# A graph convolution's sums: swapped passes, three products in the sums' banks, and steps moved to ScalarE

## The chip, the cores and the metric

The program runs on one core of a Trainium2 chip. The core has TensorE (PE in the profile, its weight loads PEld), VectorE (DVE), ScalarE (ACT), GpSimd (POOL) and SyncE (SP), each with a list of instructions of its own, worked off in order, and sixteen DMA engines that move data between memory, SBUF and PSUM. The metric is the time of one execution on the device in microseconds. The kernel before took 5058.26 us, the median of three runs from 5057.69 to 5059.12.

## The reference, cut to what matters

The reference is a network of two layers over 3125 nodes of 256 features. Each layer adds a graph convolution and a linear attention mixer to x, and then a feed-forward part. The change lies in the first layer: in its convolution, in the building of the matrix that the convolution multiplies with, and in the layer norm ahead of the first feed-forward part, which begins with a graph attention.

```python
xn = layernorm(x)
# graph convolution of layer 0: W is 256 x 256, 100000 edges src -> dst
h   = xn + segment_sum(xn[src], dst)
h   = h @ W.T + b
out = (h - mean(h, axis=0)) * rsqrt(var(h, axis=0) + 1e-5) * bn_w + bn_b
# the sum with the mixer (four blocks of attention and MLP), then the first feed-forward part
x = x + out + mixer(xn)
x = x + gat_experts(layernorm(x))    # attention over 65536 other edges gates four experts
```

## The kernel before

The sum over edges is a product with a matrix of counts. The kernel builds two such matrices in memory: `A1` in bf16, the counts of the 100000 edges, and `C2` in f32, the counts of the 65536 edges of the attention. For each column of 128 edges VectorE finds the edges that name the same entry and gives the first of them their number (`prepare`, L318 to L382, with the compares at L350 and L407), and POOL adds these values into memory by an indirect DMA (`scatter`, L418). 782 such DMAs go to `A1` and 512 to `C2`, in windows within which no entry occurs twice; a window waits for the one before. The function `both` interleaves the two lists beside the mixer. What is left of the second list is kept in `tail` and is issued after the convolution's branch (L829 and L830). A scheduler that places the instructions at compile time may set an instruction ahead of others that stand before it in the code, as long as nothing that it depends on forbids it; a block that is executed on a condition is one unit for it. `tc.no_sync_barrier()` (L791) bounds this placing and makes no engine wait.

A bf16 holds whole numbers exactly up to 256. So `prepare` also keeps, for each window, the largest value in each of two classes of edges (L365 to L378): the class is found by comparing kc/N with kc/N rounded to a whole number, and the rounding is done by adding and subtracting 8388608 (L369, L370). `at_most` (L437) turns these into a bound of the largest count, and `more` (L805 to L807) says whether it is over 256. If so, `if_more()` (L823) has the matrix counted again in f32 (`recount`) and the difference added (`residue`). With these inputs the body of the branch isn't executed; every engine still reads `more` (L787), branches, and does the bookkeeping of the semaphores that the body would have raised.

The convolution (L793 to L870) has these steps.

1. `aT`, the place of the sums (128 x 6250 f32), is filled with zeros by ScalarE (L800), `less` is the identity with its sign changed (L803), and `more` is computed.
2. The split (L809 to L821): every row of xn is written as a sum of three bf16 parts, `xb`. Part 0 is a rounded copy. For each of the next two, TensorE forms the rest in PSUM: x through the identity (L818) and minus the parts so far through `less` (L820); ScalarE rounds it (L821). A tile is 128 nodes, 25 tiles; four tiles are loaded at once, in two buffers (`rows`).
3. The branch (L823 to L828), then the tail of the second list.
4. The sums (`sums`, L726): for two passes, over the groups 0 to 2 and 3 to 6 of 512 nodes (group 6 has 53), 25 row blocks of `A1` are loaded (L743) and multiplied with the three parts (L750), one PSUM bank for each group and half of the features; group 6 has one bank for both halves. The own rows are added by a product with the identity (L757). When a pass ends, `done0` adds each sum to `aT` (L833). After both halves of a group it forms two linear products with W (L838), each of four f32 matmuls into the one bank `py`, ScalarE moves each to `yT` with the bias (L840), and VectorE takes its statistics (L842).
5. Batch norm (L846 to L870): from the statistics a scale and a shift for each feature, applied by VectorE (L865); TensorE transposes `yT` (L869), VectorE adds it to `xs` (L870). The input x was added to `xs` before (L861).

The feed-forward part follows: `normed` (L176) for groups of four tiles, with statistics on VectorE (L170, L171) and the scaling on VectorE as well (L183) unless `scalar=True` (L181, ScalarE); transposes (L195), whose result goes to SBUF by VectorE and ScalarE (L201, L199) and to memory (L953); products for the attention (L957); the first experts' products among them (L229, L931). Then the attention's logits are spread over the partitions (`asb`, L985), the rows of `C2` are loaded (`cnt`, L998), ScalarE makes penalties of them (L1002), and VectorE takes the maxima (L1005).

## Time and profile before

| what | us |
|---|---|
| median of three runs | 5058.26 |
| the profiled execution | 5066.09 |
| its span | 5064.4 |
| TensorE busy (matmuls) | 4018.7 (79%) |
| VectorE busy | 3209.6 (63%) |
| POOL busy | 2734.7 (54%) |
| ScalarE busy | 1499.4 (30%) |
| scatters into A (L418), 782 | 1224.7 busy, 1.566 each |
| scatters into C (L418), 512 | 794.2 busy, 1.551 each |
| last scatter into A starts | 2178.2 |
| last scatter into C starts | 2611.9 |
| split, first weights to last part | 2251.8 to 2291.7 |
| sums (L750), first to last matmul | 2324.7 to 2545 |
| batch norm's scaling (L865), first to last start | 2567.4 to 2581.1 |

The profile is of one execution, taken by the hardware. Busy times are sums over the span; whether an engine's time counts is seen only within its stage, by what the next instruction waits for. The rows of the table that have two times are from the span's start, so that the stages can be laid in order. A line of a timeline has the start, the length, the engine, the line of the code, the operation, what is written and read, how many instructions were merged, and in brackets the idle time of the engine ahead of it with what ended it. An engine with a q behind its name is its sequencer, which reads the list, branches and issues DMAs.

### The profile page before, as it was taken

The page shows a single profiled execution, that of the slowest core. Times are in us where ns is not written, and L with a number is a line of the kernel's source. Part 1 is how long each engine was busy: PE and PEld are TensorE (multiplying, and loading weights), DVE is VectorE, ACT ScalarE, POOL GpSimd, SP SyncE. Part 2 cuts the span into 40 slices and gives each one's busy share as a digit, 9 for nine tenths or more (in the row PEclk, how much of TensorE's full clock was granted, in tenths as well). Part 3 has the DMA queues.
Part 4 walks back from the last instruction along what each step waited for, and adds up shares of the span by engine and source line. Part 5 has one row for each costly group of instructions (what it writes and reads, how often), then busy time and mean ns, then how long its engine had stood idle before and what let it go on. Part 6 is the DMA issues. An engine that isn't in the chain of part 4 may idle for free. (4 is left out here: it accounts for less than half of the span.)

```text
span 5064.4 us, 50451 instructions
## 1 busy us (share of the span) xinstructions
PE 4018.7 (79%) x16771; PEld 2309.4 (46%) x16771; DVE 3209.6 (63%) x8299; ACT 1499.4 (30%) x2396; POOL 2734.7 (54%) x1835
## 2 busy tenths in 40 slices
PE   1477788878866786787979974766689998999999
PEld 1254455545633454453445642222345444454477
DVE  7978887888788879510048996889973031332231
ACT  0322133113211131130014448989740021000033
POOL 2578888888888888866740006888620031001034
PEclk6668887888777788888989986788899999999999
DMA  9934443444433323236546543323291212222176
GB/s 330 284 47 70 73 74 46 69 70 66 50 17 26 34 9 17 8 25 111 74 88 229 181 132 115 102 83 93 77 282 54 85 49 72 56 60 70 51 180 169
DMA packets 446886, 472.09 MB, mean 93 GB/s; under 512 B 213041, under 2 KB 354138, under 8 KB 441557
## 3 DMA queue, kind: packets, MB, share of 16 engines
q1 hardware_dynamic: 249418, 455.15, 29.5%
q0 software_dynamic: 197184, 13.47, 12.8%
q8 instruction: 140, 2.29, 0.2%
q14 instruction: 144, 1.18, 0.1%
HBM read 338.77 MB, written 130.63 MB: 93 GB/s over the span
## 5 line engine op out<-in xcount | busy, mean ns | idle before, releaser
L418 POOL DMA_INDIRECT A<-lowa,keya x782 | 1224.7, 1566 | 369.4 <-issue 219.0
L418 POOL DMA_INDIRECT C<-valb,keyb x512 | 794.2, 1551 | 220.9 <-issue 136.7
L1092 POOL TENSOR_TENSOR ex<-ex,pqb 128x1024 f32<-128x1024 f32 (+3 forms) x200 | 366.7, 1855 | 514.2 <-ACT ex L1091 514.0
L350 DVE SCALAR_TENSOR_TENSOR junk<-kr,keya,w_before 128x640 bf16<-128x640 f32 (+2 forms) x729 | 603.4, 828 | 14.7 <-DMA kr<-keys_a 3.3
L195 PE MATMUL tr<-ident,rows 128*128 128x128 f32 (+1 forms) x500 | 106.9, 369 | 506.8 <-ACT rows L181 488.7
L407 DVE SCALAR_TENSOR_TENSOR junk<-kr,keyb,w_before 128x1024 bf16<-128x1024 f32 (+1 forms) x390 | 496.2, 1272 | 17.0 <-DMA kr<-keys_b 11.0
L229 PE MATMUL mm<-hT,w 128*128 128x512 f32 (+1 forms) x896 | 423.0, 638 | 17.3 <-ACT hT L197 14.9
L750 PE MATMUL ag<-chb,Hb 128*128 128x512 bf16 (+1 forms) x1800 | 418.9, 386 | 12.3 <-DMA chb<-A 12.3
L750 PE MATMUL ag<-chb,xb 128*128 128x512 bf16 (+2 forms) x1950 | 399.6, 364 | 34.5 <-DMA chb<-A 34.0
L1005 DVE CUSTOM_DVE_ANT_0 am<-asb,pen 128x1664 f32<-128x1664 f32 (+3 forms) x200 | 357.2, 1786 | 48.0 <-ACT pen L1002 38.0
L707 PE MATMUL o<-w,hid 128*128 128x256 f32 (+1 forms) x1600 | 382.8, 393 | 0.0
L1127 PE MATMUL pa<-ex,hgp 128*32 128x512 f32 (+3 forms) x1400 | 217.6, 703 | 190.7 <-DVE ex L1115 187.4
L1115 DVE SCALAR_TENSOR_TENSOR ex<-ex,ct 128x2048 f32<-128x2048 f32 (+3 forms) x175 | 346.0, 2006 | 24.6 <-ACT ex L1108 14.1
L1108 ACT ACTIVATE ex<-ex,as 128x1024 f32<-128x1024 f32 (+3 forms) x400 | 344.8, 932 | 0.0
L707 PEld LDWEIGHTS o<-w,hid 128*128 128x128 f32 (+1 forms) x1600 | 296.9, 190 | 79.4 <-issue 36.9
L1358 POOL DMA_INDIRECT slots<-rb,r_ati x50 | 49.9, 998 | 513.0 <-DVE rb L1351 404.4
L232 ACT ACTIVATE hid<-mm,fm 128x512 f32<-128x512 f32 (+1 forms) x336 | 210.9, 631 | 372.1 <-PE mm L229 360.3
L195 PEld LDWEIGHTS tr<-ident,rows 128*128 128x128 f32 (+1 forms) x500 | 67.6, 178 | 551.4 <-ACT rows L181 521.7
L229 PEld LDWEIGHTS mm<-hT,w 128*128 128x128 f32 x896 | 193.1, 234 | 238.5 <-issue 195.7
L750 PEld LDWEIGHTS <-xb 128*128 128x128 bf16 (+1 forms) x2100 | 182.9, 97 | 252.1 <-issue 41.8
L750 PEld LDWEIGHTS <-Hb 128*128 128x128 bf16 (+1 forms) x2100 | 184.5, 99 | 225.5 <-issue 33.2
L181 ACT ACTIVATE rows<-xs,ln_nmr,rs_y 128x256 f32<-128x256 f32 (+1 forms) x200 | 105.2, 591 | 612.5 <-DVE ln_nmr L174 585.2
(441 smaller groups left out, 6754.9 us busy)
## 6 DMA issues: line engine op xcount, KB each, us to landing
C<-zero SPq DMA_DIRECT2D x25, 1528.0 KB
cnt<-C SPq DMA_DIRECT2D x24, 1562.5 KB
cd<-C SPq DMA_DIRECT2D x36, 1024.0 KB
kr<-keys_b SPq DMA_DIRECT2D x64, 512.0 KB
f1w<-in_f_w_dram SPq DMA_DIRECT2D x56, 512.0 KB
slots<-blank SPq DMA_DIRECT2D x15, 1820.0 KB
kr<-keys_a SPq DMA_DIRECT2D x48, 512.0 KB
kr<-keys_a SPq DMA_DIRECT2D x69, 320.0 KB
```

The lines of the kernel that those rows point to most:

```text
L229: T.matmul(ph[:, :n], lhsT=w1[:, k, hb * P:(hb + 1) * P], rhs=xT[:, k, :n], start=(k == 0), stop=(k == 1))
L232: S.activation(h[:, :n], ph[:, :n], AF.Gelu, bias=bias[hb])
L350: V.scalar_tensor_tensor(junk[:, :k * P], self.kr[:, at:at + k * P], key[:, c + j:c + j + 1], self.w_before[:, u:u + k * P], op0=OP.is_equ ...
L407: V.scalar_tensor_tensor(out, kk, key[:, c + j:c + j + 1], by, op0=OP.is_equal, op1=OP.mult, accum_out=more[:, j:j + 1] if i else self.val ...
L418: s = G.indirect_dma_start(out=self.flat, out_offset=bass.IndirectOffsetOnAxis(ap=self.idx[:, c:c + 1], axis=0), in_=(self.val if self.low ...
L707: T.matmul(po[:r], lhsT=hid[hb][:, j * P:j * P + r], rhs=w2[:, hb, :], start=(hb == 0), stop=False)
L750: T.matmul(acc[fb, g][:, :n], lhsT=Xb[:r, s, i, fb * P:(fb + 1) * P], rhs=ch[:r, at:at + n], start=first, stop=last, skip_group_check=g == ...
L1005: V.tensor_tensor_reduce(out=junk[:r, :w], in0=asb[:r, h, c0:c1], in1=pen[:r, :w], scale=1.0, scalar=-3.0e38, op0=OP.subtract, op1=OP.max, ...
L1092: G.tensor_tensor(e, e, pq[:r, h, :n], op=OP.add)
L1108: S.activation(ex[:r, h, :n], ex[:r, h, :n], AF.Exp, bias=sc)
L1115: V.scalar_tensor_tensor(e4, e4, 1.0, ct[:r, None, :m].to_broadcast([r, 4, m]), op0=OP.min, op1=OP.mult)
L1127: T.matmul(pa[32 * h:32 * h + 32, c:c + m], lhsT=hgp[:r, at:at + 32], rhs=ex[:r, h, c:c + m], start=(s == 0), stop=(s == NT - 1))
```

## The change

- The two rounding steps of the classes (L369, L370) are done by ScalarE, as copies with a scale and a bias.
- `at_most` uses PSUM banks with the tag `tr`, which the mixer has, and the bound is computed within the mixer: in the last block, ahead of the second group from the end (group 5). `more` is allocated earlier for it.
- The split forms the rest once for each tile. ScalarE rounds it to part 1, and VectorE subtracts part 1 from the rest in PSUM, which gives part 2. The rest has six banks and not five. `aT` is filled after the split in the code.
- The passes of the sums are swapped: groups 3 to 6 first, then 0 to 2. A linear product of the groups 0 to 2 goes to the bank that held this group's sum (`ag{hb}_{g}`), and no longer to `py`; the groups 3 to 6 still use `py`.
- Batch norm's scaling (L865) and the scaling of the layer norm ahead of the feed-forward part (L950) are done by ScalarE.

```diff
@@ -366,8 +366,8 @@
                 assert n * win == w and self.windows <= MOSTW
                 part = small.tile([P, COLS], F32, name="e_part", tag="e_part", bufs=1)
-                V.tensor_scalar(part[:, :w], kc, 1.0 / N, 8388608.0, op0=OP.mult, op1=OP.add)
-                V.tensor_scalar(part[:, :w], part[:, :w], -8388608.0, None, op0=OP.add)
+                S.activation(part[:, :w], kc, AF.Copy, scale=1.0 / N, bias=8388608.0)
+                S.activation(part[:, :w], part[:, :w], AF.Copy, bias=-8388608.0)
                 V.scalar_tensor_tensor(part[:, :w], kc, 1.0 / N, part[:, :w], op0=OP.mult, op1=OP.is_ge)
                 V.tensor_tensor(rel[:, :w], sel[:, :w], val, op=OP.mult)
                 V.tensor_tensor(part[:, :w], part[:, :w], rel[:, :w], op=OP.mult)
@@ -438,13 +438,13 @@
             top = small.tile([P, 2, 2], F32, name="e_top", tag="e_top")
             V.memset(top, 0.0)
-            q = ps.tile([P, P], F32, name="mq", tag="mq", bufs=1)
             for j in range(2):
                 for i in range(2):
                     n = min(P, MOSTW - i * P)
-                    p = ps.tile([P, P], BF16, name="mt", tag="mt", bufs=2)
-                    T.transpose(p[:n], self.most[:, j, i * P:i * P + n], ident_b)
-                    V.tensor_reduce(top[:n, i, j:j + 1], p[:n], axis=AX.X, op=OP.max)
+                    p = ps.tile([P, 1024], BF16, name="mt", tag="tr", bufs=2)
+                    T.transpose(p[:n, :P], self.most[:, j, i * P:i * P + n], ident_b)
+                    V.tensor_reduce(top[:n, i, j:j + 1], p[:n, :P], axis=AX.X, op=OP.max)
+            q = ps.tile([P, 512], F32, name="mq", tag="tr", bufs=2)
             for i in range(2):
                 T.matmul(q[:1, :2], lhsT=ones_col, rhs=top[:, i, :], start=(i == 0), stop=(i == 1))
             return q[:1, :2]
@@ -499,6 +499,7 @@
                 tail.append((c, (c - c0) % TAIL == TAIL - 1 or c == eb.made - 1))
+    more = ctile([1, 1], "more", I32)
     edge_stack = ExitStack()
     ep = edge_stack.enter_context(tc.tile_pool(name="ep", bufs=1, side="right"))
     with ExitStack() as st:
@@ -686,6 +687,11 @@
                 ts = tiles_of(g)
                 r = rows_of(ts[-1])
                 n = cols_of(g)
+                if l == LAYERS - 1 and g == NG - 2:
+                    assert ea.made == ea.width
+                    most = small.tile([1, 1], F32, name="most", tag="most")
+                    V.tensor_reduce(most, ea.at_most(ps), axis=AX.X, op=OP.max)
+                    V.tensor_scalar(more, most, MOST, None, op0=OP.is_gt)
                 qT = work.tile([P, 2, 512], F32, name="qT", tag="hT")
                 transposed(ps, qT, [Q[:r, t, :] for t in ts], r)
                 for j, t in enumerate(ts):
@@ -789,7 +795,6 @@
     tc.no_sync_barrier()
-    more = ctile([1, 1], "more", I32)
     with ExitStack() as st:
         gp = st.enter_context(tc.tile_pool(name="gnn0", bufs=1))
         wg = gp.tile([P, 2, D], F32, name="wg", tag="wg")
@@ -797,14 +802,10 @@
         aT = gp.tile([P, 2, N], F32, name="aT", tag="aT")
         yT = gp.tile([P, 2, N], F32, name="yT", tag="yT")
         stats = gp.tile([P, 2, NG, 6], F32, name="stats", tag="stats")
-        S.activation(aT, ones_col[:, 0:1, None].to_broadcast([P, 2, N]), AF.Copy, scale=0.0)
         xb = gp.tile([P, NT, 3, D], BF16, name="xb", tag="xb")
         less = gp.tile([P, P], BF16, name="less", tag="less")
         S.activation(less, ident, AF.Copy, scale=-1.0)
         with tc.tile_pool(name="ps_g0p", bufs=1, space=PSUM) as ps:
-            most = small.tile([1, 1], F32, name="most", tag="most")
-            V.tensor_reduce(most, ea.at_most(ps), axis=AX.X, op=OP.max)
-            V.tensor_scalar(more, most, MOST, None, op0=OP.is_gt)
             for t in range(NT):
                 r = rows_of(t)
@@ -813,12 +814,12 @@
                     load_rows(xg, xn_d, t // 4)
                 x = xg[:r, t % 4, :]
                 S.activation(xb[:r, t, 0, :], x, AF.Copy)
-                for i in range(2):
-                    p = ps.tile([P, D], F32, name="rest", tag="rest", bufs=5)
-                    T.matmul(p[:r], lhsT=ident[:r, :r], rhs=x, start=True, stop=False)
-                    for k in range(i + 1):
-                        T.matmul(p[:r], lhsT=less[:r, :r], rhs=xb[:r, t, k, :], start=False, stop=(k == i))
-                    S.activation(xb[:r, t, i + 1, :], p[:r], AF.Copy)
+                p = ps.tile([P, D], F32, name="rest", tag="rest", bufs=6)
+                T.matmul(p[:r], lhsT=ident[:r, :r], rhs=x, start=True, stop=False)
+                T.matmul(p[:r], lhsT=less[:r, :r], rhs=xb[:r, t, 0, :], start=False, stop=True)
+                S.activation(xb[:r, t, 1, :], p[:r], AF.Copy)
+                V.tensor_tensor(xb[:r, t, 2, :], p[:r], xb[:r, t, 1, :], op=OP.subtract)
+        S.activation(aT, ones_col[:, 0:1, None].to_broadcast([P, 2, N]), AF.Copy, scale=0.0)
         with (tc.tile_pool(name="g0t", bufs=1) as rp, tc.tile_pool(name="ps_g0t", bufs=1, space=PSUM) as ps,
               if_more()):
             def add0(g, fb, p, n):
@@ -833,7 +834,9 @@
                 V.tensor_tensor(aT[:, fb, 512 * g:512 * g + n], aT[:, fb, 512 * g:512 * g + n], p[:, :n], op=OP.add)
                 if fb:
                     for hb in range(2):
-                        py = ps.tile([P, 512], F32, name="py", tag="py", bufs=1)
+
+                        tag = f"ag{hb}_{g}" if g < 3 else "py"
+                        py = ps.tile([P, 512], F32, name="py", tag=tag, bufs=1)
                         for k in range(2):
                             T.matmul(py[:, :n], lhsT=wg[:, k, hb * P:(hb + 1) * P],
                                      rhs=aT[:, k, 512 * g:512 * g + n], start=(k == 0), stop=(k == 1))
@@ -841,7 +844,7 @@
                                      bias=fcol("gnn_b", hb))
                         V.bn_stats(stats[:, hb, g, :], yT[:, hb, 512 * g:512 * g + n])
-            sums(ps, gp, xb, 2, [[0, 1, 2], [3, 4, 5, 6]], done0, shared=NG - 1, own=ident_b)
+            sums(ps, gp, xb, 2, [[3, 4, 5, 6], [0, 1, 2]], done0, shared=NG - 1, own=ident_b)
         with tc.tile_pool(name="ps_g0b", bufs=1, space=PSUM) as ps:
             mv = small.tile([P, 2, 2], F32, name="bn_mv", tag="bn_mv")
             for hb in range(2):
@@ -862,7 +865,7 @@
                                 op=OP.add)
                 for hb in range(2):
                     y = yT[:, hb, 512 * g:512 * g + n]
-                    V.tensor_scalar(y, y, sc[:, hb:hb + 1], sh[:, hb:hb + 1], op0=OP.mult, op1=OP.add)
+                    S.activation(y, y, AF.Identity, scale=sc[:, hb:hb + 1], bias=sh[:, hb:hb + 1])
                 for j, t in enumerate(ts):
                     p = ps.tile([P, D], F32, name="trb", tag="trb", bufs=4)
                     for hb in range(2):
@@ -947,7 +950,7 @@
                 ts = tiles_of(g)
                 r = rows_of(ts[-1])
                 nx = work_rows(len(ts), r)
-                normed(nx, [xs[:r, t, :] for t in ts], r)
+                normed(nx, [xs[:r, t, :] for t in ts], r, scalar=True)
                 hT = work.tile([P, 2, 512], F32, name="hT", tag="hT")
                 transposed(ps, hT, nx, r)
                 nc.sync.dma_start(xf_d[:, :, 512 * g:512 * g + cols_of(g)], hT[:, :, :cols_of(g)])
```

## The prediction

> **What bounds the kernel now.** I read the chain of waits first. The 195 longest pieces that it lists all lie after 4222 us and belong to stages that the change leaves alone, so it prices nothing here. I then took the engines by stage from the end of the mixer (2250 us) to the attention maxima (2671 us), the timelines of each engine there, and the records of the branch (L787 and L823).
>
> Busy time by stretch (length, then PE, PE load, DVE, ACT, POOL, TensorE clock, DMA share, GB/s):
>
> ```profile
> 2249.81:2291.70 41.89, 35.24 (x183) 24.22 (x182) 1.68 (x8) 29.06 (x77) 32.04 (x21) 0.94 0.61 78
> 2291.70:2324.68 32.98, 0.00 (x0) 0.03 (x1) 2.45 (x2) 0.00 (x0) 19.31 (x13) 0.50 0.36 46
> 2324.68:2544.90 220.22, 219.61 (x1224) 104.09 (x1224) 15.45 (x21) 4.13 (x6) 161.28 (x105) 0.99 0.64 97
> ...
> 2567.37:2583.19 15.82, 12.19 (x50) 7.84 (x50) 15.21 (x40) 0.00 (x0) 13.38 (x9) 0.71 0.25 0
> 2583.19:2608.90 25.71, 13.35 (x57) 11.91 (x58) 18.75 (x105) 1.19 (x2) 19.27 (x13) 0.50 0.65 125
> 2608.90:2651.90 43.00, 42.52 (x216) 29.41 (x215) 17.40 (x92) 14.31 (x28) 2.01 (x2) 0.98 0.38 127
> ```
>
> The split into three bf16 parts takes 42 us, then TensorE does nothing for 33 us, then the sums keep it full for 220 us. The batch norm pass is DVE's (15.2 of 15.8 us) with ACT at nothing; the layer norm after it leans on DVE at first, and TensorE is full from 2609 us. What is TensorE waiting for in the 33 us? The timelines of ACT, PE, SP and POOL, and the branch's records:
>
> ```profile
> 2249.79 5.41 ACT L800 ACTIVATE aT<-ones_col 128x6250 f32<-128x6250 f32 x1 [5.36 <-PE o L221]
> 2291.32 0.38 ACT L821 ACTIVATE xb<-rest 53x256 bf16<-53x256 f32 x1 [0.89 <-PE rest L820]
> ...
> L787 POOLq TENSOR_LOAD <-more x3: 294/301/509, 2304.0 to 4219.4; - x3
> L823 PEldq COMPARE_BRANCH  x1: 4967/4967/4967, 2291.1 to 2291.1; - x1
> L823 POOLq INC_SWDGE_SEM  x1: 1567/1567/1567, 2319.8 to 2319.8; - x1
> 2315.73 1.54 POOL L418 DMA_INDIRECT C<-valb,keyb  x1 [0.30 <-issue]
> ...
> 2321.57 8.80 SPq L743 DMA_DIRECT2D chb<-A  x9
> 2324.68 5.34 PE L750 MATMUL ag<-chb,xb 128*128 128x512 bf16 x18 [33.40 <-DMA chb<-A]
> ```
>
> The last part is ready at 2291.7, but SP may load A only when POOL has passed the branch: its bookkeeping for the body not taken ends at 2319.8 + 1.57 = 2321.4, and SP starts 0.2 us later. POOL is late because the compile-time order set scatters of the second list's tail ahead of the branch, although the code has them behind it. The timeline shows them: from 2197.68 to 2315.73, windows of 16, 16, 16 and 11, 59 in all, one each 1.85 us, with 2 to 6 us between windows. So the split, drawn by the compiler, fixes the place of the branch in POOL's list, and POOL's slower real pace fixes its time. Third, the end of the sums and what sets the next stage:
>
> ```profile
> 2544.99 1.98 PE L838 MATMUL py<-aT,wg 128*128 128x512 f32 x4
> 2547.01 0.69 ACT L840 ACTIVATE yT<-py,fm 128x512 f32<-128x512 f32 x1 [102.38 <-PE py L838]
> 2547.73 0.69 DVE L842 BATCH_NORM_STATS2 stats<-yT 128x6 f32<-128x512 f32 x1 [0.97 <-ACT yT L840]
> 2563.63 0.22 DVE L842 BATCH_NORM_STATS2 stats<-yT 128x6 f32<-128x53 f32 x1 [0.45 <-ACT yT L840]
> ...
> 2611.87 1.54 POOL L418 DMA_INDIRECT C<-valb,keyb  x1 [2.51 <-DMA C<-valb,keyb]
> ...
> 2654.41 1.18 SPq L998 DMA_DIRECT2D cnt<-C  x2
> 2669.81 3.08 ACT L1002 ACTIVATE pen<-cnt,big 128x1664 f32<-128x1664 f32 x2
> ```
>
> One linear product, one eviction and one restart take 2.76 us, since all share the bank `py`: 18.9 us for seven groups. The last scatter into C starts at 2611.87, 42.5 us before SP asks for the first rows of C, so C is not late now.
>
> **What the Trainium skill says.** "Runtime: NRT & Kernel Launch", section "Instruction fetch mechanics", says that a taken branch to a page not at hand stalls for its fetch; PE's COMPARE_BRANCH of 4.97 us fits that. "ScalarE: Activation LUTs", "What ACT_TABLE_LOAD costs", prices an ACTIVATE at 186 ns + 0.833 ns per element, + 93 ns per column operand: 585 ns at 256 elements with two, where L181 shows 588. Its section "Step-by-step: what each stage is for" says that scale and bias are one fused multiply-add with a single rounding: kc/N + 8388608 then still rounds to a whole number, so the bound keeps its value. No run shows that yet. "PSUM — Partial Sum Buffer", "PSUM bank collisions raise a hardware error", demands that a product in a sum's bank wait for the add that reads it; the adds (L833, 0.68 us) are due before the product anyway.
>
> **The change part by part.**
>
> *Split.* Per tile it drops two of four f32 matmul records (L818) and two of three bf16 ones (L820) and one of three ACT copies, and adds a DVE subtract. ACT's pace was 1.06 us a tile (three copies; pairs of L821 run in 0.66, triples of L815 in 1.03); now 0.70, 17.5 us for 25 tiles instead of 26.4. DVE (0.4 us a tile, as L870) and PE (0.7) run beside it. The loads become the limit: two buffers, and 4.3 to 6.6 us from issue to use (2276.31 to 2280.7, 2258.72 to 2265.3), with 2.8 us of work on each. Walking through the six loads gives parts ready near 2250 + 26 = 2276, plus the branch's 5 us: TensorE could start at 2281. The 5.41 us fill of `aT` moves behind and is needed only at 2425.
>
> *Branch.* The 59 scatters cover 41.9 us of split. 26 us would be 37 of them, 31.4 us (the fill not hidden) 44. In the instruction order of the kernel before, ten of the 59 lie in the fill and about nine on each group of four tiles, less two at each window's end; two thirds of that for six groups gives 36 to 41, with the fill up to 51. I take 43, range 34 to 52. POOL's real time for the 43rd: the third window starts at 2262.11, its eleventh scatter ends 10 x 1.85 + 1.54 later, 2282.1. As before, 4.3 us (2317.27 to 2321.57) to SP's load and 3.1 to the first matmul: 2289.5 for 2324.7, **35 us** earlier. 34 scatters would give 2273, so TensorE's own 2281 holds (43 us); 52 give 2304.3 + 7.4 = 2311.7 (13 us).
>
> *Bound.* Four transposes, four reduces (0.28 us), two products and two steps, some 2.3 us in a row (2249.81 to 2252.27), move into the mixer's sixth group of the last layer, where DVE is 15% busy (2100 to 2250). TensorE's transposes queue behind that group's work and wait for a `tr` bank; 0 to 3 us on the mixer's end, hidden while POOL is later. It is cover for nothing else: `lowa` was complete at 1372.
>
> *Two rounding steps on ACT.* 66 DVE records of 0.17 us go (L369, L370), 33 calls. They cost DVE about 0.08 to 0.17 us each, 5 to 11 us of a mixer in which DVE is 85% busy; the mixer's end gains 0 to 8. Against it the compare (L371) now waits for ACT. ACT is usually ahead (its `lowa` waited 139.9 us for DVE between 300 and 1400), so I take nothing, from -5 to +20 on the mixer's end.
>
> *Passes swapped.* TensorE's own work is the same; the first pass's products lie among the second's matmuls as now (that stretch is full), and group 6's two small ones (1.3 us) join them. At the end six products run back to back, 24 matmuls at 0.43 us = 10.3, + 0.5 for the last add, 0.27 to fill, 0.69 eviction, 0.69 statistics: 12.5 for 18.9. Less 1.3: **5 us**, range 3 to 7.
>
> *Batch norm on ACT.* 14 records leave DVE (12 x 0.54 + 2 x 0.3 = 7 us); 25 adds at 0.35 us pace stay (9 us). ACT's price for 512 elements is 0.80 us, some 0.71 overlapped: 9.1 us, and 2 us until the first add. 12 to 13 us for 15.8: **3 us**, range 1 to 5.
>
> *Layer norm on ACT.* Some twelve rows (0.35 us pace) of the DVE part go, 4 us; ACT's rows take 0.52 us pace and delay each group's transposes. TensorE's full part behind is unmoved. **2 us**, -1 to 5.
>
> *C.* Sum 45 us. SP would then ask for C at 2609; POOL's list is the same length and still ends at 2613.4, plus 3.7 to 6.5 us as between windows: 2617 to 2620. SP is held about 9 us, but the queued broadcasts (`asb`, 6.4 MB at the 361 to 425 GB/s seen from 2650 to 2670) fill half of that. Cost 4 us, so **41 us** is left. Against the profiled 5066.1 us (span 5064.4) that is 5025; the runs' median is 7.8 us lower, and the same 41 from it gives **5017 us**. All stages after it wait in turn, so I let the shift through.
>
> **Rivals.**
> 1. *Branch still late.* 50 to 52 scatters go ahead, as loads or the fill hold the split up. 13 + 10 = 23 us: 5035. For it: two buffers; against: the fill has gaps to lie in.
> 2. *Branch count unmoved*, some other dependence places it: only the 10 us of the three later parts: 5048.
> 3. *Slower: ACT in DVE's way.* In `prepare` an ACT step sits behind an eviction that waits for TensorE, DVE stands, and the mixer ends d later. TensorE then starts at 2285 + d (26 split, 5 branch, 3 load and its first step); with 10 us gained later, it loses from d = 50, or 1.85 us for each of the 27 calls inside the mixer. ACT's waits for `mm` average 1.3 us and reach 3.2, those for `tr` 17.2; two steps at 1.5 us are 81 us: 5058 + 31 = 5089. Against: DVE is the laggard there.
> 4. *Body taken*, should the rounding differ: 782 scatters x 1.85 = 1446 us at least: above 6500.
>
> **How the numbers follow.** Forecast 0.64 (own range 5005 to 5030), rivals 0.19, 0.06, 0.08, 0.03. Faster by over 0.2% (10 us, what this measurement can tell): 0.64 + 0.19 + half of the second = 0.86; within: 0.03; slower: 0.11. The low end is 43 us at the start, 10 later and no loss on C, 5005; 5042 at the top takes in the first rival and leaves out about 0.18.
>
> **What would show it.** First sum matmul near 2289 (2281 to 2312), with about 43 scatters between 2197 and the branch; 12 to 13 us from the last sum to the last statistics; batch norm pass near 12.5 us; SP's first load of C waiting for POOL's list; mixer's end within 8 us of 2250. If TensorE starts at 2320 or later, or the mixer ends beyond 2290, the forecast is wrong.

## The result, and the profile after

The kernel after took 5017.6 us, the median of four runs from 5006.2 to 5028.4, where the kernel before took 5058.7 beside it: a ratio of 0.9916 with a 95% interval from 0.9891 to 0.9941, 41 us. A second series, of six runs, gave 0.9909, from 0.989 to 0.9928. The forecast was 5017, with 41 us.

The profiled execution took 5028.4 us (span 5026.4) at a mean TensorE clock of 0.855; it is the slowest of the four. Busy time by stretch in the kernel after, in the columns of the same view of before (length, then PE, PE load, DVE, ACT, POOL, clock, DMA share, GB/s):

```profile
2231.61:2261.60 29.99, 19.27 (x75) 12.56 (x75) 9.84 (x25) 21.26 (x51) 22.08 (x15) 0.83 0.56 102
2261.60:2271.95 10.35, 0.00 (x0) 0.02 (x1) 2.75 (x3) 0.00 (x0) 3.71 (x3) 0.57 0.59 181
2271.95:2492.20 220.25, 220.00 (x1224) 104.48 (x1225) 14.21 (x22) 4.74 (x8) 165.96 (x109) 0.99 0.61 96
2492.20:2505.85 13.65, 12.54 (x34) 5.16 (x32) 7.64 (x13) 4.12 (x6) 11.52 (x8) 1.00 0.28 0
2505.85:2520.86 15.01, 9.47 (x50) 7.25 (x50) 12.21 (x42) 9.22 (x14) 11.45 (x8) 0.77 0.28 1
2592.59:2619.08 26.49, 8.76 (x16) 3.87 (x16) 0.00 (x0) 0.69 (x1) 9.26 (x6) 0.66 0.67 195
```

The first two rows are the split and the hole behind it. The split with the fill takes 30.0 us (42 before), the hole 10.4 (33 before). The third row holds the sums, all but the last 2 us: the last sum ends at 2494.25, so they take 222.3 us (220.4 before), since two more products now lie among them. The row from 2492 is the end of the second pass: TensorE is busy 12.5 of 13.7 us there, the products run back to back (2494.18 to 2504.75). In the row from 2505.85, the batch norm pass, ScalarE now has 9.2 us of work. The last row is the one to stop at: 26.5 us just ahead of the attention in which VectorE does nothing and ScalarE almost nothing, while the DMA engines are at 0.67.

The records of the branch in the kernel after (line, engine's queue, count, duration in ns, first and last start in us):

```profile
L824 POOLq EVENT_SEMAPHORE  x4: 17/43/6568, 2260.2 to 2267.0; - x4
L824 POOLq COMPARE_BRANCH  x1: 53/53/53, 2257.1 to 2257.1; - x1
L824 PEldq COMPARE_BRANCH  x1: 4957/4957/4957, 2261.4 to 2261.4; - x1
L824 POOLq INC_SWDGE_SEM  x1: 1095/1095/1095, 2267.1 to 2267.1; - x1
```

Its timelines around the branch, of ScalarE, GpSimd, SyncE and TensorE (start, us, engine, line, instruction, and in brackets the idle time before it and what ended it):

```profile
2231.43 5.39 ACT L822 ACTIVATE aT<-ones_col 128x6250 f32<-128x6250 f32 x1
2261.16 0.38 ACT L820 ACTIVATE xb<-rest 53x256 bf16<-53x256 f32 x1 [0.18 <-PE rest L819]
...
2261.00 1.54 POOL L418 DMA_INDIRECT C<-valb,keyb  x1 [0.31 <-issue]
2268.88 1.54 POOL L418 DMA_INDIRECT C<-valb,keyb  x1 [6.34 <-DMA C<-valb,keyb]
...
2268.38 10.44 SPq L749 DMA_DIRECT2D chb<-A  x9
2271.96 1.44 PE L756 MATMUL ag<-chb,xb 128*128 128x512 bf16 x3 [10.84 <-DMA chb<-A]
```

36 scatters of the tail now stand ahead of the branch (59 before); the 36th starts at 2261.00. In before, POOL's bookkeeping ended 25 us after TensorE's branch. Here TensorE's branch ends at 2261.4 + 5.0 = 2266.4 and POOL's bookkeeping at 2267.1 + 1.1 = 2268.2: both sides arrive together, and the first sum matmul comes at 2272.0 instead of 2324.7. The fill of `aT`, which stands behind the split in the code, was still put ahead of its copies (2231.43). Within the split TensorE waits three times for the rows of xn, 5.4 us in all:

```profile
2245.26 0.67 PE L818 MATMUL rest<-xg,ident 128*128 128x256 f32 x2 [2.17 <-DMA xg<-xn_d]
...
2253.70 0.67 PE L818 MATMUL rest<-xg,ident 128*128 128x256 f32 x2 [2.18 <-DMA xg<-xn_d]
...
2257.12 0.67 PE L818 MATMUL rest<-xg,ident 128*128 128x256 f32 x2 [1.01 <-DMA xg<-xn_d]
```

Last, what stands ahead of the attention, in the timelines of GpSimd, SyncE and ScalarE of the same kernel:

```profile
2583.22 1.54 POOL L418 DMA_INDIRECT C<-valb,keyb  x1 [0.31 <-issue]
2597.95 1.54 POOL L418 DMA_INDIRECT C<-valb,keyb  x1 [13.18 <-DMA C<-valb,keyb]
...
2609.30 1.54 POOL L418 DMA_INDIRECT C<-valb,keyb  x1 [2.42 <-DMA C<-valb,keyb]
...
2578.47 1.85 SPq L988 DMA_DIRECT2D asb<-as_d  x3
...
2592.03 0.51 SPq L988 DMA_DIRECT2D asb<-as_d  x1
2592.59 0.95 SPq L928 DMA_DIRECT2D xfg<-xf_d  x1
2612.26 0.80 SPq L1001 DMA_DIRECT2D cnt<-C  x2
...
2619.08 3.09 ACT L1005 ACTIVATE pen<-cnt,big 128x1664 f32<-128x1664 f32 x2 [11.82 <-DMA cnt<-C]
```

SyncE is done with its broadcasts at 2593.5 and then stands until 2612.26, 18.7 us, because `C` is complete only behind the scatter of 2609.30. The second list is now the limit. One of its windows, issued up to 2584.8, held POOL for 13.2 us instead of the usual 2 to 6 (the tail's first window waited 14.6 us, long before this, as it does for 10 to 15 in every profile; no run here explains that): the window lies beside the four broadcasts `asb`. The first maximum starts at 2620.8, 50.7 us earlier than in before; the first sum stood 52.7 us earlier, and the late parts should have added to that.

From the logits of the attention on, both kernels have the same instructions in the same order. What the first profile of after loses behind 2620.8 (span 38 us shorter, not 51) is therefore put down to no edit: the second profile of the same kernel, below, keeps its 52.6 us at the first maximum to the end (span 52.9 us shorter).

### The profile page after: what moved, and what is told of

The parts are those of the page before. It is cut to its first block, busy times and chain, and to the rows that moved or that the text cites. A ratio compares the mean times of both kernels' runs of the same rounds, so it can differ in the third digit from the quotient of the medians.

```text
span 5026.4 us, 50136 instructions
## 1 busy us (share of the span) xinstructions
PE 4005.7 (80%) x16671; PEld 2300.2 (46%) x16671; DVE 3203.9 (64%) x8219; ACT 1526.5 (30%) x2476; POOL 2735.4 (54%) x1835
## 5 line engine op out<-in xcount | busy, mean ns | idle before, releaser
L350 DVE SCALAR_TENSOR_TENSOR junk<-kr,keya,w_before 128x640 bf16<-128x640 f32 (+2 forms) x729 | 603.6, 828 | 13.6 <-DMA kr<-keys_a 2.2
L181 ACT ACTIVATE rows<-xs,ln_nmr,rs_y 128x256 f32<-128x256 f32 (+1 forms) x225 | 118.6, 591 | 546.8 <-DVE ln_nmr L174 513.7
```

What stands on the lines that cost most here:

```text
L350: V.scalar_tensor_tensor(junk[:, :k * P], self.kr[:, at:at + k * P], key[:, c + j:c + j + 1], self.w_before[:, u:u + k * P], op0=OP.is_equ ...
```

## The experiments

Two statements were to be tested. The first: the gain comes from the count of scatters that the compile-time order sets ahead of the branch, not from TensorE being done sooner. The second: what the late parts win (own banks, batch norm and layer norm on ScalarE) is given back where `C` is late. The rival to the first is that TensorE's split set the start; to the second, that the parts simply add up.

Single profiles, some of them from different chips, differ by ten microseconds and more at the mixer's end, so the table has differences within one execution beside the times. "Mixer" is the start of the mixer's last add, "A" of the last scatter into the first matrix, "sums" of the first sum matmul, "C" of the last scatter, "max" of the first attention maximum; all in us of the profile. The ratio is to the kernel before on the same chip.

| kernel | mixer | A | sums | C | max | sums − A | max − sums | ratio, 95% interval |
|---|---|---|---|---|---|---|---|---|
| before | 2249.8 | 2178.2 | 2324.7 | 2611.9 | 2671.5 | 146.5 | 346.8 | 1 |
| after | 2231.2 | 2171.0 | 2272.0 | 2609.3 | 2620.8 | 101.0 | 348.8 | 0.9916, 0.9891 to 0.9941 |
| after_2 | 2238.5 | 2164.1 | 2279.3 | 2590.3 | 2618.9 | 115.2 | 339.6 | 0.9909, 0.989 to 0.9928 |
| late_parts | 2233.8 | 2175.1 | 2319.8 | 2602.9 | 2659.8 | 144.7 | 340.0 | 0.9987, 0.9981 to 0.9994 |
| round_only | 2226.6 | 2164.2 | 2305.8 | 2592.4 | 2652.6 | 141.6 | 346.8 | 0.9995, 0.9984 to 1.0006 |
| split_bound | 2238.9 | 2170.6 | 2277.0 | 2599.0 | 2628.5 | 106.4 | 351.5 | 0.9914, 0.9901 to 0.9928 |
| no_late_parts | 2236.8 | 2172.1 | 2274.9 | 2607.7 | 2624.0 | 102.8 | 349.1 | 0.992, 0.9903 to 0.9938 |
| count59 | 2235.2 | 2183.3 | 2324.2 | 2612.6 | 2664.9 | 140.9 | 340.7 | 0.9979, 0.9967 to 0.9991 |
| old36 | 2234.7 | 2178.0 | 2282.2 | 2605.0 | 2630.0 | 104.2 | 347.8 | 0.9926, 0.9911 to 0.994 |
| c_short | 2239.0 | 2178.6 | 2279.6 | 2577.1 | 2619.1 | 101.0 | 339.5 | 0.9893, 0.9877 to 0.9909 |
| asb_half | 2231.5 | 2171.0 | 2272.7 | 2603.3 | 2614.7 | 101.7 | 342.0 | 0.9909, 0.9892 to 0.9926 |
| asb_after | 2225.6 | 2173.4 | 2269.4 | 2599.5 | 2611.1 | 96.0 | 341.7 | 0.99, 0.9882 to 0.9917 |
| fill_dve | 2233.8 | 2171.5 | 2270.0 | 2606.2 | 2617.6 | 98.5 | 347.6 | 0.9908, 0.9888 to 0.9928 |
| pair3_7 | 2215.4 | 2268.1 | 2290.5 | 2614.3 | 2628.3 | 22.4 | 337.8 | 0.9919, 0.9901 to 0.9937 |

**split_bound: the split, the fill's place and the bound alone.** The kernel before with these three edits; the diff is that of the change without its first, fourth and later parts (rounding, banks, passes, both norms).

> The kernel before with the new split, the fill of aT behind it and the bound inside the mixer; rounding on VectorE, passes and norms as before. 36 scatters stand ahead of the branch. Theory 1 (the split gives the gain at the start, bounded by the mixer's end when the rounding is not moved): last add of the mixer at 2247 to 2252, split's end 25 to 27 us later, first sum matmul at 2284 to 2292 (33 to 41 us earlier than before), the list's end no later than 2618, so little wait for it; total 5018 to 5026. Rival (the count of scatters alone sets the start, as in the profile of after where both ended together): first sum matmul at 2272 to 2280, and the list's end then costs some of it; total 5010 to 5018.

The ratio is 0.9914, all of the change's gain. The sums start 106.4 us after the first list's end and 38.1 after the mixer's; the expected 2284 to 2292 assumed a mixer's end near 2250, which this execution didn't have. Its 2277.0 lies in the rival's range, but not for the rival's reason: POOL's bookkeeping was done at 2264.4, and SyncE's load came at 2273.69, behind the end of TensorE's branch (2272.3), so the split was the later side.

**late_parts: only what comes after the sums begin.**

```diff
-                        py = ps.tile([P, 512], F32, name="py", tag="py", bufs=1)
+                        tag = f"ag{hb}_{g}" if g < 3 else "py"
+                        py = ps.tile([P, 512], F32, name="py", tag=tag, bufs=1)
...
-            sums(ps, gp, xb, 2, [[0, 1, 2], [3, 4, 5, 6]], done0, shared=NG - 1, own=ident_b)
+            sums(ps, gp, xb, 2, [[3, 4, 5, 6], [0, 1, 2]], done0, shared=NG - 1, own=ident_b)
...
-                    V.tensor_scalar(y, y, sc[:, hb:hb + 1], sh[:, hb:hb + 1], op0=OP.mult, op1=OP.add)
+                    S.activation(y, y, AF.Identity, scale=sc[:, hb:hb + 1], bias=sh[:, hb:hb + 1])
...
-                normed(nx, [xs[:r, t, :] for t in ts], r)
+                normed(nx, [xs[:r, t, :] for t in ts], r, scalar=True)
```

> The kernel before with the swap of the passes, the three groups' own banks, and the batch and layer norm steps on ScalarE; split, branch, bound and rounding as before. Theory 1 (the parts are worth what the trace of after shows, 5 + 4.7 + 2.4 us, and here nothing takes them back, since the second edge list ends 42 us before its rows are asked for): first sum matmul unmoved at 2324.7, maxima 11 to 13 us earlier than 2671.5, total 5045 to 5048. Rival (the passes' end and the norms are covered by something else when they stand alone): maxima within 4 us of 2671.5, total 5055 to 5059.

The first maximum comes 340.0 us after the first sum matmul instead of 346.8, and the time falls by 6.4 us (5059.2 to 5052.8). The stretches of this kernel for the pass's end and the batch norm:

```profile
2540.20:2553.90 13.70, 12.63 (x34) 5.21 (x32) 7.69 (x13) 4.13 (x6) 11.54 (x8) 1.00 0.23 0
2553.90:2568.90 15.00, 9.42 (x50) 7.24 (x50) 12.24 (x42) 9.22 (x14) 10.80 (x7) 0.77 0.21 1
```

These are the rows of after. From the first sum matmul to the start of the last statistics it is 233.83 us (238.95 before), from there to the start of the last add of the batch norm 15.3 (19.1). From that add to the first broadcast it is 61.0 (60.4): the layer norm on ScalarE gives nothing; and from the first broadcast to the first maximum 30.0 (28.3), while SyncE now issues the last broadcast 13.6 us after the first instead of 9.6. So 5.1 + 3.8 − 0.6 − 1.6 = 6.7, well below the expected 11 to 13. One more thing is in this profile. Up to the branch the kernel has exactly the instructions of before, and yet its mixer ends at 2233.8 instead of 2249.8. (The two profiles may be of different chips.) The 18.6 us by which the mixer of after ended earlier are thus no evidence for the change.

**round_only: the two rounding steps alone.** The kernel before with

```diff
-                V.tensor_scalar(part[:, :w], kc, 1.0 / N, 8388608.0, op0=OP.mult, op1=OP.add)
-                V.tensor_scalar(part[:, :w], part[:, :w], -8388608.0, None, op0=OP.add)
+                S.activation(part[:, :w], kc, AF.Copy, scale=1.0 / N, bias=8388608.0)
+                S.activation(part[:, :w], part[:, :w], AF.Copy, bias=-8388608.0)
```

> The kernel before with the two rounding steps on ScalarE alone. 59 scatters still stand ahead of the branch. Theory 1 (these steps bring the mixer's end forward by 18 us and GpSimd's first list by 7): last add of the mixer at 2231 to 2236, last scatter into A at 2170 to 2173, first sum matmul 7 us earlier (2317 to 2319), as the scatters and not the mixer set it; total 5050 to 5053. Rival (the mixer gained by the bound's new place or by another order of the instructions, not by the rounding): last add at 2247 to 2252, first sum matmul within 2 us of 2324.7, total 5056 to 5060.

Its one profile looks like theory 1 (mixer's end at 2226.6), but the time doesn't: 0.9995, with an interval from 0.9984 to 1.0006, so between 8 us gained and 3 lost. With the finding just above, the profile can't carry it. Nor can the time: with 59 scatters ahead of the branch GpSimd is the later side, so a mixer that ends earlier is covered, and the 7 us that theory 1 gives the first list lie within the interval. Whether the rounding is worth anything is left open.

**no_late_parts: after without the late parts.** The diff of late_parts, backwards, on the kernel after.

> The kernel after with swap, own banks, and both norm steps undone; split, branch, bound and rounding stay. Theory 1 (in after, the second edge list's end at 2609 sets the start of the attention, so the late parts are idle time there): SP asks for the first counts some 11 us later than in after but still has to wait for the list or finds it just done, maxima within 3 us of after's 2620.8, total within 4 us of after's 5017. Rival (the parts add up as my sum had it, the list costing 4 us): maxima at 2630 to 2633, total 5027 to 5030.

The time is theory 1's (5019.4), and SyncE did wait for `C`, as its timeline and GpSimd's show:

```profile
2607.66 1.54 POOL L418 DMA_INDIRECT C<-valb,keyb  x1 [9.86 <-DMA C<-valb,keyb]
...
2601.95 1.47 SPq L986 DMA_DIRECT2D asb<-as_d  x2
2603.46 0.57 SPq L926 DMA_DIRECT2D xfg<-xf_d  x1
2615.76 0.80 SPq L999 DMA_DIRECT2D cnt<-C  x2
```

SyncE stood 11.7 us, until 8 us after the list's last scatter had started; that scatter itself had waited 9.9 us for the window ahead of it, which lay beside the broadcasts. Little of this was lost, since the counts then came 6.5 us after they were asked for (15.4 in before, where they follow the broadcasts at once). The first maximum, 2624.0, is 3.2 us behind that of after (theory 1: within 3), and the distance from sums to maximum is 349.1, near that of the other kernels without late parts (346.8, 346.8, 347.8, 351.5). The first profile of after has the same distance, 348.8, with the late parts in it: in that execution they bought nothing.

**after_2: the kernel after once more.**

> The kernel after once more, as the measure for the two beside it and for how far one profile differs from the next: first sum matmul 99 to 103 us after the last scatter into A and first maximum 346 to 351 us after the first sum matmul, while the mixer's end itself may lie anywhere from 2226 to 2250; total 0.989 to 0.994 of before.

The distance sums to maximum isn't 346 to 351 but 339.6, the value of late_parts, so here the late parts count in full. Its timelines of GpSimd, SyncE and ScalarE show why:

```profile
2574.56 1.66 POOL L418 DMA_INDIRECT C<-valb,keyb  x1 [0.30 <-issue]
2579.06 1.54 POOL L418 DMA_INDIRECT C<-valb,keyb  x1 [2.84 <-DMA C<-valb,keyb]
2590.30 1.54 POOL L418 DMA_INDIRECT C<-valb,keyb  x1 [2.31 <-DMA C<-valb,keyb]
...
2588.75 1.82 SPq L988 DMA_DIRECT2D asb<-as_d  x3
2602.32 0.51 SPq L988 DMA_DIRECT2D asb<-as_d  x1
2603.86 1.16 SPq L1001 DMA_DIRECT2D cnt<-C  x2
...
2617.19 3.08 ACT L1005 ACTIVATE pen<-cnt,big 128x1664 f32<-128x1664 f32 x2
```

The first list ended at 2164.1, 7 us earlier than in the first profile, and the mixer 7 us later. The last full window then ended ahead of the broadcasts and held the next for 2.8 us, not 13.2, and SyncE asked for `C` without waiting for it. The counts, right behind the broadcasts, took 13.3 us to come (2603.86 to 2617.19); in the first profile, asked for late, 6.8 (2612.26 to 2619.08). So about half of the 18.7 us that SyncE stood there was no loss: 348.8 − 339.6 is 9.2. `C` is a limit in one profile of after and not in the other, with 14 us between them in the relation of two chains: GpSimd's lists and the mixer. Expected also was a start of the sums 99 to 103 us after the first list; it was 115.2, since this time the split was the later one (40.8 us after the mixer's last add, as in the first profile).

**c_short: one window of the second list less.**

```diff
-        for c, end in tail:
+        for c, end in tail[:80] + tail[96:]:
             eb.scatter(c, end)
```

> The kernel after with one window of 16 scatters (the 81st to 96th of the tail) left out, so that C lacks their edges. Theory 1 (in after, the end of the second list starts the attention): the list ends about 33 us earlier, SP asks for the first counts right behind its broadcasts, first maximum 334 to 338 us after the first sum matmul (after: 348.8), total 5003 to 5008. Rival (the broadcasts of asb or something else would hold the attention there anyway): 346 to 349 us, total 5015 to 5020.

339.5 us from sums to maximum: with a list that ends at 2577.1 the wait is gone, and what is left is the distance of late_parts and after_2, not the expected 334 to 338. SyncE asks for the counts right behind its broadcasts (2604.53), so these hold the attention from there on, as the rival has it, at a shorter distance than it gave. The ratio is 0.9893 (this chip's kernel before took 5067.6, so that the expected times are to be read as ratios, 0.989 to 0.990); its interval overlaps those of after.

**count59: the change with the old count.** The lines for 59 scatters are written ahead of the convolution, and a bound for the scheduler keeps the others behind the branch.

```diff
+    for c, end in tail[:59]:
+        eb.scatter(c, end)
     tc.no_sync_barrier()
...
-        for c, end in tail:
+        tc.no_sync_barrier()
+        for c, end in tail[59:]:
             eb.scatter(c, end)
```

> The kernel after with 59 scatters of the tail written ahead of the branch, and a barrier of the scheduler so that no other goes ahead of it; all of the change stays, the quick split too. Theory 1 (the count of scatters ahead of the branch set the start of the sums, TensorE's quicker split alone buys nothing): first sum matmul 140 to 147 us after the last scatter into A (before: 146.5, after: 101.0), total 5050 to 5054, the late parts' 6 us. Rival (the split's own time set it): 101 to 115 us, total 5015 to 5028.

0.9979, and 140.9 us from the first list to the sums: of the gain no more is left than the late parts can account for (0.9987 in late_parts, and the intervals overlap). The records of its branch:

```profile
L824 PEldq COMPARE_BRANCH  x1: 3892/3892/3892, 2263.5 to 2263.5; - x1
L824 POOLq COMPARE_BRANCH  x1: 53/53/53, 2304.2 to 2304.2; - x1
L824 POOLq INC_SWDGE_SEM  x1: 1567/1567/1567, 2319.1 to 2319.1; - x1
```

TensorE has passed the branch at 2267.4; SyncE's load comes at 2320.90, behind POOL's bookkeeping (2319.1 + 1.6), and TensorE stands 57 us. The quick split of TensorE buys nothing here.

**old36: the old split with the new count.** The same edit on the kernel before, with 36.

> The kernel before, old split and all, with 36 scatters of the tail written ahead of the branch and a barrier of the scheduler behind them. Theory 1 (two limits: GpSimd's count, and behind it TensorE's split): now the split, 42 us from the mixer's end, sets the start, with 8 us for branch and load: first sum matmul 48 to 54 us after the mixer's last add and 110 to 120 us after the last scatter into A, total 5026 to 5034. Rival (the count alone): 101 to 105 us after the last scatter into A, total 5017 to 5023. If the split were all: 140 us and more, 5055 and more.

0.9926: 37 us (30 to 45 by the interval) come with the old split. Here TensorE is the later side, by its branch:

```profile
L825 POOLq INC_SWDGE_SEM  x1: 1095/1095/1095, 2267.1 to 2267.1; - x1
L825 PEldq COMPARE_BRANCH  x1: 5877/5877/5877, 2276.0 to 2276.0; - x1
```

The sums start at 2282.2, 0.3 us after that branch, 104.2 after the first list, at the rival's end of the range and below the 110 to 120 expected; 47.5 after the mixer's last add, near the 48 to 54. The mixer of this execution was early against its first list, so the split cost less. The time, 5021 by the ratio, is in the rival's range too. What the quicker split adds beyond the count isn't shown: 0.9914 (split_bound) and 0.9926 have overlapping intervals.

**pair3_7: three scatters of the second list between those of the first, in its last seven chunks.**

```diff
-                if c + k < c1 and (k > PAIR or (c + k - c0) % WIDE == 0):
+                if c + k < c1 and (k > 3 or (c + k - c0) % (4 * k) == 0):
...
+            pair = 3 if i >= len(chunks) - 7 else PAIR
             if paired:
-                yield from eb.prepare(PAIR * len(ws), PAIR)
+                yield from eb.prepare(pair * len(ws), pair)
...
-                    for j in range(PAIR):
+                    for j in range(pair):
...
+        tc.no_sync_barrier()
         for c, end in tail:
```

> The kernel after with three scatters into C instead of two between those into A in the last seven chunks: 45 scatters of the second list move out of the tail, where each window waits for the one before, into the first list, and a barrier keeps the tail behind the branch. Theory 1 (the second list's end is the limit in after, and GpSimd has time before the branch): last scatter into A 80 to 88 us later than in after, first sum matmul within 6 us of after's 2272, list's end 10 to 20 us earlier, first maximum 336 to 342 us after the first sum matmul (after: 348.8), total 5004 to 5012. Rival (the later end of the first list makes the branch late, or the mixer slower): first sum matmul 2280 or later, total 5017 to 5030.

The rival's outcome: the first list ends 97 us later, not 80 to 88, TensorE's split was done near 2246, but POOL came to the branch only at 2269.9 and was through its bookkeeping at 2287.0, and the second list ends at 2614.3, no earlier than in after (2609.3). 0.9919, no better than after.

**asb_half and asb_after: the broadcasts moved.** In asb_half the second halves of the columns are loaded behind the first counts. In asb_after, whose edit is shown, all eight halves are written behind them, and the compiled order put one ahead again.

```diff
-            for h in range(4):
-                nc.sync.dma_start(asb[:, h, :], as_d[h:h + 1, :].to_broadcast([P, N]))
...
                         nc.sync.dma_start(cnt[q0:q1], C22[t * P + q0:t * P + q1, :])
+                    if t == 0:
+                        for c0, c1 in ((0, MID), (MID, N)):
+                            for h in range(4):
+                                nc.sync.dma_start(asb[:, h, c0:c1], as_d[h:h + 1, c0:c1].to_broadcast([P, c1 - c0]))
```

> The kernel after with the four broadcasts asb loaded in two halves of the columns, the second half behind the loads of the first counts. Theory 1 (the broadcasts, 6.4 MB in some 14 us, hold up the window of scatters that falls beside them, 13.2 us instead of 2 to 6, and so the second list's end, which is the limit): that wait falls to 5 to 9 us, first maximum 341 to 346 us after the first sum matmul (after: 348.8), total 3 to 7 us below after. Rival (the window's wait has another cause, or the second half comes too late for the maxima): wait stays over 11 us, or the maxima of the first tile take over 20 us; total within 2 us of after or above it.

> The kernel after with the four broadcasts asb in eight half pieces, seven of them behind the loads of the first counts, so behind the second list's end. Theory 1: the window's wait falls to 2 to 6 us, the list ends 325 to 329 us after the first sum matmul (after: 337.3), first maximum 337 to 343 us after it; the first tile's eight maxima then wait for pieces of 0.85 MB and take 15 to 20 us instead of 14.8; total 4 to 9 us below after. Rival (the pieces come too late and cost what the list gains): first tile's maxima take 25 us or more, total within 2 us of after or above it.

The window's wait is 8.8 us in asb_half and 2.8 in asb_after (the next, of five scatters, 5.8), where it was 13.2 in after: it falls with the part of the broadcasts that lies beside it, so they are what holds it. The maxima start 342.0 and 341.7 us after the sums. The times are those of after, 0.9909 and 0.99, with overlapping intervals: no gain is shown. The profile of asb_half keeps its lead at the second tile of the maxima (356.8 us after the sums; in after 363.7), and where the time loses it isn't shown. In asb_after the timeline of VectorE has part of the reason:

```profile
2624.10 1.68 DVE L1010 CUSTOM_DVE_ANT_0 am<-asb,pen 128x1461 f32<-128x1461 f32 x1
2630.79 1.89 DVE L1010 CUSTOM_DVE_ANT_0 am<-asb,pen 128x1664 f32<-128x1664 f32 x1 [5.01 <-ACT pen L1007]
```

The first tile's eight maxima run without a gap, in 14.7 us, but the second tile's counts come behind the broadcasts, and 5.0 us go there. The second tile begins 361.4 us after the sums: of 7.1 us at the first maximum 2.3 are left.

**fill_dve: the fill of `aT` off ScalarE.**

```diff
-        S.activation(aT, ones_col[:, 0:1, None].to_broadcast([P, 2, N]), AF.Copy, scale=0.0)
+        V.memset(aT, 0.0)
```

> The kernel after with the fill of aT on VectorE instead of ScalarE, where in after it still runs ahead of the split's copies (5.4 us). Theory 1 (the start of the sums is the later of two: TensorE's side, 40.8 us after the mixer's last add in two profiles of after, fill, split, branch and load in a row; GpSimd's side, 96 to 101 us after the last scatter into A): TensorE's side falls to 34 to 37 us, and the first sum matmul stands there or 96 to 105 us after the last scatter into A, whichever is later; total within 5 us below after. Rival (the loads of the rows or VectorE's subtracts set the split's pace, so that the fill was covered): first sum matmul 40 us or more after the mixer's last add even where that is more than 105 us after the last scatter into A; total as after.

37 scatters are ahead of the branch here. Theory 1: the sums start 36.2 us after the mixer's last add (40.8 before the edit), 98.5 after the first list, so both sides are again together. The window beside the broadcasts waits 13.35 us here too, sums to maximum is 347.6, and the time is that of after, 0.9908. What may have been won at the start doesn't reach the attention.

## Why the prediction was right

The total was right, and so was the order of the causes: the count of scatters ahead of the branch first, the late parts second, `C` as the counterweight. Of the terms, several were off, and that their errors cancelled to the microsecond is luck.

- *Split.* 26 us were predicted; from the fill's end at 2236.7 to the last part at 2261.6 it is 25. The size was right, the reason only in part: the loads, named as the limit, cost TensorE 5.4 us in three waits, and most of the rest is its own work (19.3 us busy of the 30). And "TensorE could start at 2281", 31 us after the mixer, left out two terms: the fill didn't move behind the split in the compiled order (5.4 us), and from the end of TensorE's branch to the first matmul there are 5.6 us more, in which SyncE's load of `A` is issued and lands (2266.4 to 2272.0). 5.4 + 25 + 5 + 5.6 is 41; 40.8 was measured, and 36.2 without the fill.
- *Branch.* 43 scatters were taken, range 34 to 52; it was 36. The start at 2289.5 became 2272.0. Against before's own profile that is 52.7 us, but before's profile had the latest mixer of all fourteen. The means are the better measure: 2318.6 over the four kernels with 59 scatters ahead, 2275.0 over the seven with 36, the new split and the fill on ScalarE, so 43.6 us where 35 was predicted; by the distances from the last scatter into A the same eleven profiles give 40.0. count59 and old36 show that it is the count. That TensorE's being done sooner is not what matters was the step that decided, and it held. Why the count falls is argued: each kernel with the new split has 36 or 37 ahead, each with the old one 59, unless it was set by hand, which fits a scheduler that draws the split shorter; but no run has the new split without the bound's move. The change turned a chain with one late side into one with two equal sides, so more speed on TensorE's side brings little (fill_dve: 98.5 us from the first list instead of 101.0).
- *Bound.* 0 to 3 us on the mixer's end, hidden. Nothing of it is seen in any profile, nor could be, with the mixer's end at 2225.6 to 2239.0 in the kernels that have it in the loop (pair3_7, whose lists are spread otherwise, apart).
- *Rounding.* "I take nothing" stands within what round_only can tell. In every kernel with the rounding on ScalarE the branch's body stayed out, which would have cost 1446 us at least. That fits the single rounding that the Trainium skill states ("ScalarE: Activation LUTs", "Step-by-step: what each stage is for") but doesn't test it: no run shows the rounded values.
- *Swap and banks.* 5 us predicted; to the start of the last statistics it is 5.1 in late_parts and 5.4 in after. The statistics now follow each other every 1.72 us instead of 2.76.
- *Batch norm.* 3 us predicted, 3.8 in late_parts. In after an ACTIVATE on 512 elements lasts 0.80 us and the next starts 0.71 us after it; that is the price in the Trainium skill ("ScalarE: Activation LUTs", "What ACT_TABLE_LOAD costs"), 0.80 less an overlap of 0.09 back to back, from which 0.71 was taken.
- *Layer norm.* 2 us predicted, range −1 to 5. In late_parts it is −0.6 to the first broadcast, inside the range; from there to the first maximum another 1.6 are lost, perhaps by the new order of SyncE's issues, and with them it is −2.2, below the range.
- *C.* 4 us were predicted as its cost. In two profiles of the kernel with the change's late parts (after, fill_dve) it is 8 to 9 (348.8 and 347.6 against 339.6), in a third nothing. That SyncE's wait is half filled by the queued broadcasts held (18.7 us stood, 9.2 lost). My sum let the waiting window wait 3.7 to 6.5 us "as between windows"; that it would lie beside the broadcasts, which the change brings to the same time, and then wait 13, was not seen. The time of no_late_parts (0.992) beside the two series of after (0.9916 and 0.9909) says how little of the late parts' 6.4 us is left; the intervals are too wide for a number.

The sum of the measured terms: 40.0 or 43.6, + 6.8 for the late parts, less some 0 to 9 at `C`, is 38 to 50; the two series give 42.5 (0.84%) and 46 (0.91%) of 5058.7. Of the predicted 35 + 10 − 4 the first term was too small, the second too large, and the third too small where the window falls beside the broadcasts.

Of the rivals, the first (50 to 52 scatters ahead) is out with 36, the fourth with a body that isn't executed. count59 is the second (count unmoved, 5048): brought about by hand, with the late parts in place, it gave 0.9979, which is 5048 of 5058.7. The third, ScalarE in VectorE's way in `prepare`, would have needed a mixer 50 us longer; none was.

## What to carry to other kernels

When a conditional block stands between two streams of work, look in the compiled order at what was set ahead of it on each engine: with 59 scatters of 1.85 us ahead on GpSimd, TensorE's own speed there was worth nothing, and 23 fewer were worth 37 us without any other edit. Two chains that meet (here the lists on GpSimd and the mixer) shifted against each other by 10 us and more from one profile to the next, so compare distances within one profile and take times for the verdict, and don't read an edit's effect from the absolute place of a landmark. When a stage is brought forward, ask which of its transfers now falls beside another engine's chain of waits: here broadcasts of 6.4 MB lengthened one such wait from 3 to 13 us.

## What the runs showed of the hardware

- A window of indirect scatters waited 13.2 and 13.35 us for the one before it when broadcasts had been issued shortly before that one's end (after, fill_dve), 8.8 with half of them (asb_half), and 2.8 with none (asb_after, after_2).
- The first counts came 13.3 us after they were asked for when they stood right behind the broadcasts (after_2), and 6.8 when they were asked for 18.7 us after the broadcasts (after).
- With the same instructions in the same order on TensorE, VectorE, ScalarE and GpSimd up to the first sum, the mixer's last add came at 2249.8 in one profile (before) and at 2233.8 in another (late_parts).
- TensorE's branch over the body not taken took 3.67 to 5.88 us in the fourteen profiles, 4.94 to 4.99 in eight of them; those of GpSimd took 0.05.
